# VectorE copies 24 columns of x per group instead of 12

## The chip, the core and the metric

The kernel runs on one core of a Trainium2 chip. The core has a matrix engine (TensorE, PE in the profile), a vector engine (VectorE, DVE), an activation engine (ScalarE, ACT), a general engine (GpSimd, POOL) and a queue engine (SyncE, SP). Each has its own instruction stream and they meet only at semaphores. The metric is device time in microseconds, from the first to the last instruction plus a little around them.

## What is computed

One graph layer with attention on edges, a batch norm and a layer norm. There are N = 12,500 nodes with 128 features and E = 212,500 edges, sorted by destination:

```python
Q, K, V = x @ WQ, x @ WK, x @ WV            # seen as 8 heads of 16
Eh = edge_attr @ WE
score = exp(clip(sum_over_head(K[src] * Q[dst] / 4 * Eh), -5, 5))
wV = segment_sum(V[src] * score, dst);  Z = segment_sum(score, dst)
h = x + wV / (Z + 1e-6)
y = batch_norm_over_nodes(h) * gamma + beta
out = layer_norm_over_features(x + y)
```

## The kernel before

The edges are cut into 1661 tiles of 128. Eight tiles make a group, and there are 208 groups. A window of 64 nodes holds the destinations of four tiles, so Q is not gathered: a 64-column piece of x is multiplied by WQ and spread to the edges with a one-hot matrix.

K and V of the sources do need a gather. At the start the kernel makes a table `kvd` of K and V for all nodes in DRAM (256 floats a row). For each tile, POOL issues one indirect DMA (L290, queue POOL) that brings 128 rows of it into the tile's part of a slot `slot` (9 slots of 8 tiles). Some groups have one tile, the eighth, that comes another way, and POOL then issues seven gathers for the group:

- 61 tiles by ACT: x lies transposed in SBUF as `hx`, one node a column. ACT copies 40 single columns a group (L393) into `xc`, PE multiplies 128 collected columns by `w_kv` (`cols_mm`, L430), ACT copies the product into the slot (`cols_out`, L435).
- 24 tiles by SP: 16 row DMAs a group (L411), copied into the slot by ACT (L421).
- 18 tiles by VectorE: 12 single columns a group (L366) into `xv`, and the same PE and ACT steps as for ACT's columns.

The column numbers are ids in SBUF (`v_ids`). One instruction of the sequencer (`load_v`, L357, TENSOR_LOAD in the profile) loads 12 of them into registers of VectorE; in front of every copy stands one register instruction (`ISA` in the program's order, FUSED_REGOPS in the profile) that turns a node number into an address. `v_plan` says at which groups a tile is collected and multiplied (`v_at`), and into which group's slot it goes (`v_tiles`).

The order of work is written out by hand: the program is one loop over groups g, and each engine runs its instructions in that order. On VectorE the order of a group is: four products K·Eh and ·Q (L800, two halves of four tiles each), the head sums (L807), the clip (L816), the one-hot of group g+2 (L748), three steps on group g-2 (L852, L855, L859), the one-hot of g+1 (L740, L741), and the message V·score (L822), which waits for ACT's exponential (L817), which waits for the clip. The 12 copies stand after L822. The id load stands between L807 and L816.

PE runs the edge products (L775), the spread of Q (L784), the sums over destinations (L843) and some small ones. POOL's gathers are issued in order; `pace` ties each to a step of the other engines, so that they are spread over a group. A gather into a slot can be issued once the message of the group that had the slot is done.

Of the kernel before, what the change touches and what calls it, by code (L numbers as in the profile page):

```python
# [15 lines left out]
ET = mybir.EngineType  # L16
# [22 lines left out]
FIRST_COL = 8  # L39
# [2 lines left out]
FIRST_ROW = 8  # L42
ROW_LAG = 2
NSEM = 6
V_COLS = 12


LAST = [3, 2]
# [51 lines left out]
def v_plan(sizes):  # L100
    full, used = sizes.count(U) // 2, set(col_plan(sizes) + row_plan(sizes))
    tiles, at, end = [], [], P
    while True:
        m = FIRST_COL + -(-end // V_COLS)
        while (m - FIRST_COL) * COLS % P < COLS:
# [17 lines left out]
def gnn_kernel(  # L123
# [19 lines left out]
    nc = tc.nc  # L143
    N, D = out.shape
# [131 lines left out]
    def slot(i):  # L276
        return rows.tile([P, 2 * G * P], F32, name=f"slot{i}")

    first = slot(NSLOT).rearrange("p (h c d) -> p h c d", h=2, d=2 * P)
# [21 lines left out]
    def issue(n=0):  # L301
        while len(queued) > n:
            f, *a = queued.pop(0)
            f(*a)
# [20 lines left out]
    tot_v = len(v_tiles) * P  # L325
    apart = set(col_tiles + row_tiles + v_tiles)
    v_ids = consts.tile([P, 2 * V_COLS], I32, name="v_ids")
    nc.vector.memset(v_ids, 0)
# [10 lines left out]
    def load_ids(to, n, first, total):  # L339
        m, rest = divmod(total, n)  # L340
        for p, k, w in ((0, m, n), (m, 1, rest)):
            if w and k:
                nc.sync.dma_start(to[p:p + k, :w], bass.AP(
                    tensor=rsrc.tensor, offset=rsrc.offset + first + n * p, ap=[[n, k], [1, w]]))

    def load_col_ids():
        load_ids(col_ids, 2 * COLS, 0, tot)
        load_ids(row_ids, 2 * SP_ROWS, tot, tot_rows)
        load_ids(v_ids, 2 * V_COLS, tot + tot_rows, tot_v)

    OFFV = {}

    def load_v(g):
        q = g - FIRST_COL
        if 0 <= q < -(-tot_v // V_COLS):
            at = q % 2 * V_COLS
            _, OFFV[g] = nc.values_load_multi_w_load_instructions(  # L357
                v_ids[q // 2:q // 2 + 1, at:at + V_COLS], engines=(ET.DVE,), min_val=0, max_val=N - 1,
                skip_runtime_bounds_check_because="node ids")

    def fetch_v(g):
        for r, off in zip(range((g - FIRST_COL) * V_COLS, tot_v), OFFV.get(g, ())):
            k = r // P
            if r % P == 0:
                XV[k] = wp.tile([P, P], F32, name="xv", bufs=2)
            nc.vector.tensor_copy(XV[k][:, r % P:r % P + 1], hx[:, ds(off, 1)])  # L366
# [8 lines left out]
    def load_cols(g):  # L375
        q = g - FIRST_COL
        if 0 <= q < -(-tot // COLS):
            at = q % 2 * COLS // 2
            _, words = nc.values_load_multi_w_load_instructions(
                col_pairs[q // 2:q // 2 + 1, at:at + COLS // 2], engines=(ET.Activation,), min_val=0,  # L380
                max_val=(N << 16) - 1, skip_runtime_bounds_check_because="node ids")
            OFFS[g] = [e for w in words for e in (w % (1 << 16), w >> 16)]
# [16 lines left out]
    def fetch_rows(g):  # L399
        q = g - FIRST_ROW  # L400
        if not 0 <= q < tot_rows // SP_ROWS:
            return
        c = q % 2 * SP_ROWS
        _, offs = nc.values_load_multi_w_load_instructions(
            row_ids[q // 2:q // 2 + 1, c:c + SP_ROWS], engines=(ET.SP,), min_val=0,
            max_val=(N - 1) * 8 * P, skip_runtime_bounds_check_because="node ids")
        for r, off in enumerate(offs, q * SP_ROWS):
            k = r // P
            if r % P == 0:
                BY_ROW[k] = late[0].tile([P, 2 * P], F32, name="byrow", bufs=2)  # L410
            d = nc.sync.dma_start(BY_ROW[k][r % P:r % P + 1, :].bitcast(U8), kvb[ds(off, 8 * P)].unsqueeze(0))  # L411
            d.then_inc(rows_in[k % NSEM], 16)
            tc.no_tile_sem_insts.add(d.ins.name)
            tc.add_to_no_dep_group(f"rows{k}", d.ins)
# [78 lines left out]
    def within(f, g):  # L493
        return f(g) if 0 <= g < NG else None
# [100 lines left out]
    def load_quad(q):  # L595
        t = late[0].tile([P, RQ, U * P], U8, name="rbq", bufs=2)
        for h in (0, 1):
            nc.sync.dma_start(t[h * WN:(h + 1) * WN].rearrange("p a b -> p (a b)"), places(h, RQ * q, RQ))
        for k in range(RQ):
            RB[RQ * q + k] = t[:, k, :]  # L600
# [93 lines left out]
    EA, OH, OT, XW, BASE, MSG, QE, OS, AT, AGG = ({} for _ in range(10))  # L694
# [4 lines left out]
    def halves(g):  # L699
        return [(0, usizes[2 * g]), (usizes[2 * g], nt(g))]  # L700

    def load(i):
        gs = range(2 * i, min(2 * i + 2, NG))
        if not gs:
            return
        t, n = wp.tile([P, 2, G, P], F32, name="ea", bufs=2), sum(nt(g) for g in gs)
        assert nt(2 * i) == G or len(gs) == 1
        for k, g in enumerate(gs):
            EA[g] = t[:, k]
        nc.sync.dma_start(t.rearrange("p c a b -> p (c a b)")[:, :n * P],  # L710
                          eaT[:, starts[2 * i] * P:(starts[2 * i] + n) * P])
# [83 lines left out]
    def products(g, hs=(0, 1)):  # L795
        for of in (EH, QE):
            for i in hs:
                a, b = halves(g)[i]
                kv = KV[g](a, b, 0)
                step = nc.vector.tensor_tensor(kv, kv, of[g][i][:, :b - a, :], op=OP.mult)  # L800
                PARTS.setdefault(g, []).append(step)

    def scores(g, h=None):
        if not h:
            SS[g] = wp.tile([P, G, H], F32, name="s", bufs=1)
        for a, b in ranges(g, h):
            step = nc.vector.tensor_reduce(SS[g][:, a:b, :], KV[g](a, b, 0).rearrange("p t (h d) -> p t h d", d=DH),  # L807
                                           axis=AX.X, op=OP.add)
        PARTS.setdefault(g, []).append(step)
# [128 lines left out]
    for q in range(NQ):  # L938
# [5 lines left out]
        for g, a in piece.get(q, []):  # L944
            if a == 0:
                i = free.pop(0)
# [62 lines left out]
    def share(g):  # L1009
        denom(g)  # L1010
        recip(g)
        attn(g)

    for g in range(NG - 2):
        within(load_rel, g + 3)
        if (g + 6) % RQ == 0 and (g + 6) // RQ in quads:
            load_quad((g + 6) // RQ)
        fetch_rows(g)
        if g % 2:
            load((g - 1) // 2 + 2)  # L1020
        within(products, g)
        within(scores, g)
        load_v(g)
        load_cols(g)
        fetch_cols(g, 0)
        within(clip_exp, g)
        within(turned_onehot, g + 2)
        if g >= 2:
            share(g - 2)
        late_x = g + 1 < nxg and g + 1 not in SLOT  # L1030
        if late_x:
            turn_x(g + 1, 0, True)
            turn_x(g + 1, 4, True)
            project_main(g + 1)
        within(eh_mm, g + 1)
        within(qe_mm, g + 1)
        cols_mm(g)
        paced = g >= LATE + 4
        if not paced:
            issue()  # L1040
        else:
            issue(G)
            for step in (SENT[g - 1], PARTS[g][1], BY["eh", g + 1], PARTS[g][3], PARTS[g][4], BY["qe", g + 1]):
                pace(step)
        within(onehot, g + 1)
        if paced:
            pace(BY["one", g + 1])
        within(message, g)
        fetch_cols(g, 1)
        within(q_window, g + 4)  # L1050
        cols_out(g)
        rows_out(g)
        fetch_v(g)
        within(add_x, g - 3)
        within(q_mm, g + 3)
        within(gather_sum, g - 1)
        if paced:
            pace(BY["sum", g - 1])
        within(x_out, g - 3)
        within(q_out, g + 3)  # L1060
        within(sums_out, g - 1)
        if g == 2:
            load_last()
            nc.vector.tensor_scalar(row_ids, row_ids, 8 * P, None, op0=OP.mult)
            pack_ids()
        if g % (RUN // 2) == 2 and g > 2 and (g // (RUN // 2) + 1) * SEC < T:
            load_section(g // (RUN // 2) + 1)
        for i, r in enumerate(runs):
            if i and g == placed[i]:
                place(r)  # L1070
        within_checks(g)
        while free and todo and todo[0] in done and not pending:
            load_x()
        bn_parts(2 * g - 7, 2 * g - 5)
        if g == NG - 4:
            assert done >= set(range(NPRE))
            norm_first()
        if g == LATE - 1:
            tps.close()
            late.append(tps.enter_context(tc.tile_pool(name="late", bufs=1)))  # L1080
        if g == LATE - 2:
            free.append(NSLOT)
            load_kv()
    last = NG - 1
    g = last - 1
# [336 lines left out]
```

## Time and profile before

| | us |
|---|---|
| median of 3 runs (lowest, highest) | 2026.02 (2023.14, 2029.82) |
| the profiled execution | 2024.75 |
| its span, first to last instruction | 2022.9 |
| busy: PE, PE's weight load, DVE, ACT, POOL | 1609.2, 1308.4, 1648.2, 1467.7, 1511.8 |
| mean granted clock of TensorE | 0.869 |

The profile gives, for each engine, the time in which it had an instruction in work. Register instructions, id loads and semaphore waits are not counted as busy, but a query of a line shows them (DVEq and ACTq are the sequencers of VectorE and ScalarE: the part that reads the instruction stream and hands instructions to the engine). In a timeline a row gives the start, the length and, in brackets, how long the engine had been idle and what ended that. A row of a line gives the count, the shortest, median and longest duration in ns, and the first and last start in us.

### The profile page before, as it was taken

The numbers are of one execution on the slowest core, as the hardware profiler recorded it, in microseconds if no ns is written. First come the engines' busy times: TensorE is split into PE (matmuls) and PEld (weight loads), VectorE is DVE, ScalarE is ACT, GpSimd is POOL, SyncE is SP. The second block draws the span as 40 slices with busy tenths as digits, with TensorE's granted clock in tenths as the row PEclk, the third lists the DMA queues.
The fourth block names the chain that finished last, engine by engine and source line by source line (L and its number), as shares of the span: only waits on it lengthen the run. The fifth ranks groups of instructions, "written<-read, shape, count | busy, mean of one in ns | idle before, by whom it ended". The sixth has DMA issues, their size and how long they took to land.

```text
span 2022.9 us, 65020 instructions
## 1 busy us (share of the span) xinstructions
PE 1609.2 (80%) x12891; PEld 1308.4 (65%) x12891; DVE 1648.2 (81%) x5264; ACT 1467.7 (73%) x9850; POOL 1511.8 (75%) x1594
## 2 busy tenths in 40 slices
PE   7888778887778887877888787778777777877787
PEld 7777666666666666665666666666566565665666
DVE  4468889889888988887888888788878788878887
ACT  2236878888788888777777777777777777777736
POOL 7677777777777777777777777777777777777765
PEclk9899888889888888888888888788888888888889
DMA  7855556556555656556656556556556556555664
GB/s 264 303 172 184 180 177 195 177 186 199 173 187 178 197 186 191 177 165 186 186 166 186 183 165 192 180 178 190 165 180 186 169 180 187 165 181 183 199 220 130
DMA packets 132237, 376.51 MB, mean 186 GB/s; under 512 B 37251, under 2 KB 50222, under 8 KB 117998
## 3 DMA queue, kind: packets, MB, share of 16 engines
q0 software_dynamic: 73760, 200.12, 33.8%
q1 hardware_dynamic: 54876, 171.03, 24.5%
q14 instruction: 312, 2.56, 0.4%
q8 instruction: 103, 1.69, 0.3%
q10 hardware_dynamic: 3186, 1.13, 0.2%
HBM read 346.69 MB, written 25.44 MB: 184 GB/s over the span
## 4 chain that ended last, share of the span: by engine, by line
issue 22%; DMA 19%; DVE 19%; PE 16%; ACT 15%; POOL 4%; ACTq 2%; DVEq 1%; SPq 1%; POOLq 0%
DMA slot<-kvd,srcs 17%; ACT xc L393 10%; DVE slot L800 7%; DVE s L807 5%; POOL slot L290 4%; PE ps_q L784 4%; PE ps_e L775 3%; PE ps_a L843 2%; DVE xv L366 2%; ACT ring L886 2%; DVE ot L748 1%; PE ps_e L487 1%; PE ps_q L910 1%; PE ps_e L910 1%; DVEq L366 1%
## 5 line engine op out<-in xcount | busy, mean ns | idle before, releaser
L290 POOL DMA_INDIRECT slot<-kvd,srcs x1494 | 1421.9, 952 | 459.9 <-issue 283.4
L393 ACT ACTIVATE xc<-hx 128x1 f32 x7808 | 1073.3, 201 | 248.2 <-issue 215.5
L775 PE MATMUL ps_e<-w_e,ea 128*128 128x128 f32 x3322 | 524.7, 313 | 269.7 <-DVE slot L800 209.1
L775 PEld LDWEIGHTS ps_e<-w_e,ea 128*128 128x128 f32 x3322 | 458.3, 216 | 335.3 <-DVE slot L800 243.5
L784 PE MATMUL ps_q<-qs,ot 64*128 64x128 f32 x3322 | 358.0, 340 | 84.6 <-DVE slot L800 74.2
L784 PEld LDWEIGHTS ps_q<-qs,ot 64*128 64x128 f32 x3322 | 294.6, 234 | 138.2 <-DVE slot L800 121.0
L800 DVE TENSOR_TENSOR slot<-slot,ps_e 128x512 f32<-128x512 f32 x410 | 268.1, 679 | 141.5 <-DMA slot<-kvd,srcs 125.0
L843 PE MATMUL ps_a<-msg,oh 128*64 128x136 f32 x3322 | 305.1, 307 | 1.7 <-DVE msg L822 1.7
L822 DVE TENSOR_TENSOR msg<-slot,ps_m 128x1024 f32<-128x1024 f32 (+2 forms) x209 | 248.7, 1191 | 34.9 <-ACT ps_m L817 32.6
L807 DVE TENSOR_REDUCE s<-slot 128x64 f32<-128x1024 f32 (+1 forms) x208 | 249.9, 1202 | 18.3 <-DVE slot L800 0.5
L800 DVE TENSOR_TENSOR slot<-slot,ps_q 128x512 f32<-128x512 f32 x410 | 261.6, 678 | 1.0 <-PE ps_q L784 0.7
L843 PEld LDWEIGHTS ps_a<-msg,oh 128*64 128x64 f32 x3322 | 194.5, 145 | 83.9 <-issue 61.6
L366 DVE COPY xv<-hx 128x1 f32 x2304 | 155.8, 143 | 0.0
L741 DVE TENSOR_TENSOR oh<-ps_i,rel 128x512 f32<-128x512 f32 x208 | 141.8, 682 | 0.0
L886 ACT ACTIVATE ring<-ps_a 128x64 f32 x408 | 90.5, 222 | 67.8 <-PE ps_a L843 46.4
L729 ACT ACTIVATE xw<-hx 128x64 f32 x416 | 83.6, 248 | 50.9 <-issue 36.3
L868 PE MATMUL ps_a<-ident,at 128*128 128x128 f32 x408 | 107.0, 350 | 1.2 <-ACT os L848 1.2
L817 ACT ACTIVATE ps_m<-s 128x64 f32<-128x64 f32 (+1 forms) x209 | 45.0, 215 | 76.6 <-DVE s L816 75.2
L868 PEld LDWEIGHTS ps_a<-ident,at 128*128 128x128 f32 x408 | 81.5, 227 | 28.3 <-issue 5.4
L748 DVE TENSOR_SCALAR ot<-rbq,wiota 128x512 f32<-128x512 uint8 x188 | 94.8, 504 | 0.0
L758 PE MATMUL ps_a<-w_q,xw 128*128 128x128 f32 x416 | 91.7, 307 | 0.4 <-ACT qs L762 0.4
L869 PE MATMUL ps_a<-xw,ident 128*128 128x128 f32 x408 | 90.8, 309 | 0.0
(188 smaller groups left out, 1492.2 us busy)
## 6 DMA issues: line engine op xcount, KB each, us to landing
ea<-eaT SPq DMA_DIRECT2D x103, 1024.0 KB
byrow<-kvd SPq DMA_DIRECT2D x3072, 1.0 KB
slot<-kvd,srcs POOLq DMA_INDIRECT x1494
rbq<-relT SPq DMA_DIRECT2D x94, 128.0 KB
kvd<-slot SPq DMA_DIRECT2D x12, 512.0 KB
kvd<-t SPq DMA_DIRECT2D x12, 512.0 KB
ring<-xT SPq DMA_DIRECT2D x24, 256.0 KB
hT<-ring SPq DMA_DIRECT2D x23, 256.0 KB
```

The costliest lines, as they stand in the source:

```text
L290: return nc.gpsimd.indirect_dma_start(out=out, out_offset=None, in_=table, in_offset=bass.IndirectOffsetOnAxis(ap=part(SRC, e, 1), axis=0))
L366: nc.vector.tensor_copy(XV[k][:, r % P:r % P + 1], hx[:, ds(off, 1)])
L393: nc.scalar.activation(XC[k][:, r % P:r % P + 1], column(at), AF.Copy)
L741: by(("one", g), nc.vector.tensor_tensor(one, iota_ps[:, None, :WN].to_broadcast([P, k, WN]), r[:, :, None].to_broadcast([P, k, WN]), op=O ...
L775: by(("eh", g), nc.tensor.matmul(t[:, j - a, :], EA[g][:, j, :], w_e, start=True, stop=True))
L784: by(("qe", g), nc.tensor.matmul(QE[g][h][:, j, :], OT[g][r, j * P:(j + 1) * P], QS[g][r], start=True, stop=True))
L800: step = nc.vector.tensor_tensor(kv, kv, of[g][i][:, :b - a, :], op=OP.mult)
L807: step = nc.vector.tensor_reduce(SS[g][:, a:b, :], KV[g](a, b, 0).rearrange("p t (h d) -> p t h d", d=DH), axis=AX.X, op=OP.add)
L822: step = nc.vector.tensor_tensor(MSG[g][:, a:b, :P].rearrange("p t (h d) -> p t h d", d=DH), KV[g](a, b, P).rearrange("p t (h d) -> p t h ...
L843: by(("sum", g), nc.tensor.matmul(AGG[g][h * WN:(h + 1) * WN], OH[g][h * n + j], MSG[g][:, h * n + j, :], start=(j == 0), stop=(j == k - 1)))
L868: nc.tensor.matmul(ps, AT[g], ident, start=True, stop=False)
L886: nc.scalar.activation(ring[:, ds(at, WN)], new, AF.Copy)
```

## The change

Three things are changed. `V_COLS` goes from 12 to 24, so that VectorE collects 24 columns in each of groups 8 to 199, and 36 tiles come in this way. The ids are loaded by two loads of 12 (`V_LOAD`); each stands right behind one of the two ·Q products, where before one stood behind the head sums. The copies stand in two batches of 12: one in the old place after the message, and a new one between the one-hot of g+2 and the steps on g-2.

```diff
-V_COLS = 12
+V_COLS = 24
+V_LOAD = 12
...
-    def load_v(g):
+    def load_v(g, half):
...
-            at = q % 2 * V_COLS
-            _, OFFV[g] = nc.values_load_multi_w_load_instructions(
-                v_ids[q // 2:q // 2 + 1, at:at + V_COLS], engines=(ET.DVE,), min_val=0, max_val=N - 1,
+            at = q % 2 * V_COLS + half * V_LOAD
+            _, OFFV[g, half] = nc.values_load_multi_w_load_instructions(
+                v_ids[q // 2:q // 2 + 1, at:at + V_LOAD], engines=(ET.DVE,), min_val=0, max_val=N - 1,
...
-    def fetch_v(g):
-        for r, off in zip(range((g - FIRST_COL) * V_COLS, tot_v), OFFV.get(g, ())):
+    def fetch_v(g, half):
+        first = (g - FIRST_COL) * V_COLS + half * V_LOAD
+        for r, off in zip(range(first, tot_v), OFFV.get((g, half), ())):
...
                 PARTS.setdefault(g, []).append(step)
+                if of is QE and len(hs) == 2:
+                    load_v(g, i)
...
         within(scores, g)
-        load_v(g)
         load_cols(g)
         fetch_cols(g, 0)
         within(clip_exp, g)
         within(turned_onehot, g + 2)
+        fetch_v(g, 0)
...
-        fetch_v(g)
+        fetch_v(g, 1)
```

The first place is on VectorE, in one group of the steady loop. Before, its order from the last products to the message is this (`ps_q` holds the spread Q, `s` the head sums, `ot`/`oh` one-hots):

```order
L800 TENSOR_TENSOR slot_22670<-slot_22670,ps_q 128x4x128 x2
L807 TENSOR_REDUCE s<-slot_22670 128x64
L357 TENSOR_LOAD v_ids
L816 TENSOR_SCALAR s<-s 128x64
L748 TENSOR_SCALAR ot<-rbq,wiota 128x512
L852 TENSOR_SCALAR rz<-os 128x8
L855 RECIPROCAL rz<-rz 128x8
L859 SCALAR_TENSOR_TENSOR at<-os,keep,rz 128x128
L740 TENSOR_TENSOR oh<-rel,lim 128x1
L741 TENSOR_TENSOR oh<-ps_i,rel 128x512
```

The same piece of a group after the change (line numbers are 2 to 4 higher; the pair of ISA and COPY, shown once, stands there 12 times):

```order
L802 TENSOR_TENSOR slot_25802<-slot_25802,ps_q 128x4x128
L358 TENSOR_LOAD v_ids
L802 TENSOR_TENSOR slot_25802<-slot_25802,ps_q 128x4x128
L358 TENSOR_LOAD v_ids
L811 TENSOR_REDUCE s<-slot_25802 128x64
L820 TENSOR_SCALAR s<-s 128x64
L750 TENSOR_SCALAR ot<-rbq,wiota 128x512
L368 ISA
L368 COPY xv<-hx 128x1
...
L856 TENSOR_SCALAR rz<-os 128x8
```

One load behind the head sums has become one behind each product, and 12 copies with 12 register instructions have come in ahead of the steps on g-2.

The second place is on POOL, at the gathers of groups 14 to 19, one row a group. Before:

```order
L290 DMA slot_1111<-kvd,srcs 128x256 x7
L290 DMA slot_1337<-kvd,srcs 128x256 x8
L290 DMA slot_1402<-kvd,srcs 128x256 x8
L290 DMA slot_1675<-kvd,srcs 128x256 x7
L290 DMA slot_1928<-kvd,srcs 128x256 x7
L290 DMA slot_2181<-kvd,srcs 128x256 x8
```

and after:

```order
L291 DMA slot_1111<-kvd,srcs 128x256 x7
L291 DMA slot_1337<-kvd,srcs 128x256 x8
L291 DMA slot_1402<-kvd,srcs 128x256 x7
L291 DMA slot_1712<-kvd,srcs 128x256 x7
L291 DMA slot_2001<-kvd,srcs 128x256 x7
L291 DMA slot_2291<-kvd,srcs 128x256 x8
```

The third row has gone from eight gathers to seven: group 16 is the first of the 18 that now get their eighth tile from VectorE's columns. Nothing else moves on POOL.

## The prediction

> **What bounds the kernel now.** I read the busy shares first, then the gathers of POOL over the whole span, then VectorE's waits by stretch, then one group of VectorE instruction by instruction. The page's shares do not name a bound:
>
> ```profile
> span 2022.9 us, 65020 instructions
> PE 1609.2 (80%) x12891; PEld 1308.4 (65%) x12891; DVE 1648.2 (81%) x5264; ACT 1467.7 (73%) x9850; POOL 1511.8 (75%) x1594
> ```
>
> POOL's 75% is misleading. Its gathers as a line (median ns, first and last start), and three of them in a timeline, with VectorE's 12 copies of that moment:
>
> ```profile
> L290 POOL DMA_INDIRECT slot<-kvd,srcs x1494: 940/946/1211, 90.0 to 1966.1; - x187
> ...
> 1013.23 0.94 POOL L290 DMA_INDIRECT slot<-kvd,srcs  x1 [0.30 <-issue]
> ...
> 1014.47 0.81 DVE L366 COPY xv<-hx 128x1 f32 x12
> 1014.47 0.94 POOL L290 DMA_INDIRECT slot<-kvd,srcs  x1 [0.30 <-issue]
> ...
> 1015.72 0.94 POOL L290 DMA_INDIRECT slot<-kvd,srcs  x1 [0.30 <-issue]
> ```
>
> A gather starts every 1.25 us. (1966.1 - 90.0) / 1493 = 1.257 us is the mean over the whole kernel, so POOL issues without a break from 90 us to 1966 us. That is the bound today. A group has 1494 / 207 = 7.22 gathers, 9.0 us. VectorE's side shows when this began to bite (70 messages from 300 to 900 us; then waits as total, times, longest, in 300 to 900 us; last row the same wait in 900 to 1900 us):
>
> ```profile
> L822 DVE TENSOR_TENSOR msg<-slot,ps_m x70: 1207/1220/1223, 302.8 to 899.7; 128x1024 f32<-128x1024 f32 x70
> DVE msg L822 <- ACT ps_m L817: 18.2, 32, 1.0
> DVE stats L889 <- ACT ring L886: 16.9, 8, 2.5
> DVE slot L800 <- DMA slot<-kvd,srcs: 6.3, 2, 4.1
> DVE relrow L583 <- PE ps_a L581: 4.6, 4, 2.0
> ...
> DVE slot L800 <- DMA slot<-kvd,srcs: 114.3, 62, 5.1
> ```
>
> Up to 900 us a group takes (899.7 - 302.8) / 69 = 8.65 us: the compute engines use up the lead of filled slots, and VectorE hardly waits for a gather. After that it waits 114.3 us for gathers. So POOL's lead over VectorE is small: 8.65 against 9.0. Without its four waits (46.0 us, 0.67 a group) VectorE needs **7.98 us a group** for its own chain. That is the number the change adds to.
>
> **The change part by part.**
>
> *Gathers.* 18 fewer at 1.25 us are 22.5 us off POOL; a group then has 1476 / 207 = 7.13, so 8.91 us. This is the whole possible gain, and it arrives only while VectorE's group stays under 8.91 us.
>
> *Where the new instructions fall.* One group of VectorE, and the records of its sequencer in the same group:
>
> ```profile
> 488.52 1.22 DVE L822 TENSOR_TENSOR msg<-slot,ps_m 128x1024 f32<-128x1024 f32 x1 [0.86 <-ACT ps_m L817]
> 489.66 0.81 DVE L366 COPY xv<-hx 128x1 f32 x12
> 490.38 1.27 DVE L800 TENSOR_TENSOR slot<-slot,ps_e 128x512 f32<-128x512 f32 x2
> 491.58 1.27 DVE L800 TENSOR_TENSOR slot<-slot,ps_q 128x512 f32<-128x512 f32 x2
> 492.95 1.22 DVE L807 TENSOR_REDUCE s<-slot 128x64 f32<-128x1024 f32 x1
> 494.21 0.19 DVE L816 TENSOR_SCALAR s<-s 128x64 f32<-128x64 f32 x1
> 494.32 0.48 DVE L748 TENSOR_SCALAR ot<-rbq,wiota 128x512 f32<-128x512 uint8 x1
> 494.71 0.37 DVE L852 TENSOR_SCALAR rz<-os 128x8 f32<-128x8 f32 x1
> ...
> 496.48 1.22 DVE L822 TENSOR_TENSOR msg<-slot,ps_m 128x1024 f32<-128x1024 f32 x1
> ```
>
> ```profile
> L366 DVEq FUSED_REGOPS  x12: 46/46/46, 488.5 to 489.8; - x12
> L366 DVE COPY xv<-hx x12: 143/144/146, 489.7 to 490.3; 128x1 f32 x12
> ...
> L800 DVEq EVENT_SEMAPHORE  x2: 21/21/21, 491.1 to 491.7; - x2
> L800 DVE TENSOR_TENSOR slot<-slot,ps_q x2: 677/678/679, 491.6 to 492.2; 128x512 f32<-128x512 f32 x2
> ...
> L357 DVEq TENSOR_LOAD <-v_ids x1: 870/870/870, 493.0 to 493.0; - x1
> ```
>
> Three things are to be seen. Copies run at a pitch of (490.3 - 489.7) / 11, about 0.06 us, but the sequencer prepares them at (489.8 - 488.5) / 11, about 0.115 us each. In the old place this is hidden: it prepares them from 488.5 on, while L822 runs for 1.22 us. And it starts on them only at 488.5, when L822 was released after 0.86 us of waiting for ACT: it does not run ahead past an instruction whose wait is open.
>
> *The old batch* stays as it is, under L822: no cost beyond what is in the 7.98.
>
> *The new batch* stands behind L816 and L748. L816 is released by L807's end, 494.21. The register work can begin about 0.1 us later, and its twelfth piece is done at 494.31 + 11 x 0.115 + 0.05 = 495.62, the copy starts at about 495.67. L852, which stood at 494.71, follows a copy's pitch later at 495.73: **+1.02 us**. The bounds: 12 x 0.06 = 0.73 if preparation were free; 12 x 0.115 = 1.38 if L816 and L748 hid nothing. I take 1.02, because both instructions (0.5 us up to L852) do hide the first four or five pieces. What may hide more is the wait for ACT's exponential, at L822 behind it (18.2 us in 70 groups, 0.26 a group): it goes, and is left out below.
>
> *The two loads.* Today's load takes 0.87 us wholly under L807 (1.22 us). What a load does to an engine's stream when nothing covers it is shown on ACT, whose load of 20 words stands behind short instructions:
>
> ```profile
> L379 ACTq TENSOR_LOAD <-col_pairs x1: 1298/1298/1298, 1017.9 to 1017.9; - x1
> ...
> 1018.08 0.29 ACT L848 ACTIVATE os<-ps_a 128x136 f32<-128x136 f32 x1
> 1019.38 0.77 ACT L393 ACTIVATE xc<-hx 128x1 f32 x5 [1.01 <-issue]
> ```
>
> What was handed over before (L848) still runs, the next waits until the load ends at 1019.2. On VectorE the first product's wait is passed at 491.1, its start is 491.58; the load lasts from about 491.19 to 492.06, the second product is due at 492.18 and is handed over in time: almost nothing lost. Its own load then runs from about 492.22 to 493.09, and the head sums start near 493.22 in place of 492.95: **+0.27 us**. Bounds: 0 if the sequencer ran ahead further, and 2 x (0.87 + 0.09) - 1.37 = 0.55 if each load began only with its product's start (0.09 is the step around a load, 1.37 the distance from 491.58 to 492.95). I take 0.27, since the wait at 491.1 is a row and not a guess. The removed load at L807 gives nothing back: L816 has to wait for L807 anyhow.
>
> *PE and ACT* get 18 more column products, in two parts of about 0.48 us each, and 18 copies of 0.384 us:
>
> ```profile
> L430 PE MATMUL ps_e<-w_kv,xv x36: 379/483/793, 260.1 to 1924.2; 128*128 128x256 f32 x36
> ...
> L435 ACT ACTIVATE slot<-ps_e x79: 384/384/386, 207.5 to 1950.3; 128x256 f32<-128x256 f32 x79
> ```
>
> That is 7 us of ACT and under 18 us of PE over 192 groups. I cost them at nothing: a longer VectorE group leaves both idle for 0.7 us or more a group. If that cover were gone they would cost 0.04 and 0.09 us a group.
>
> *Waits that stay.* Each of the 8 statistics steps waited 2.1 us for ACT's writes. Of that 1.02 goes to the new batch, and 0.3 because ACT, no longer late, starts at once: 0.8 x 8 / 69 = 0.09, with the 4.6 / 69 = 0.07 of L583 it is 0.16 us a group. The gather wait goes.
>
> **The sum.** A group of VectorE: 7.98 + 1.02 + 0.27 + 0.16 = 9.43 us, which is over POOL's 8.91. VectorE becomes the bound, and POOL, whose next gather needs a slot that VectorE has left, waits. Before, the groups that copy took (first and last copy of
>
> ```profile
> L366 DVE COPY xv<-hx x2304: 135/143/151, 172.3 to 1907.0; 128x1 f32 x192
> ```
>
> less 0.7 for the last batch itself) 1734.0 / 191 = 9.08 us. So 192 x (9.43 - 9.08) = +67 us. The last eight groups copy nothing and find their gathers done: they lose the late gather wait, 114.3 us over the 107 groups (1000 us / 9.36) of 900 to 1900 us, 1.07 each, -8.6 us. Net +58.6 us. The profiled execution took 2024.75 us, 1.85 more than its span and 1.3 under the median of the runs; put on the median, 2026.0 + 58.6 = **2085 us**.
>
> **The rivals.**
>
> *Faster: POOL stays the bound.* If VectorE's sequencer prepared copies and loaded ids past an open wait, the new batch would be ready when L807 ends and cost 0.73, the loads nothing. 7.98 + 0.73 + 0.16 = 8.87 us is under 8.91, and the gain of 22.5 us arrives: 2003 us. It decides at 8.91 - 8.14 = 0.77 us of new time a group. The rows at 488.5 speak against it: 0.86 us of open wait, and no preparation in it. [...]
>
> *Slower still: each load begins with its product.* 0.55 in place of 0.27 is 192 x 0.28 = +54 us, 2139 us. It holds if the wait of the first product is passed late, as where PE is behind; against it, the group above.
>
> [...] If copies held up POOL's gathers, each new batch would add up to 0.81 us to POOL's 8.91: 9.72 us, and POOL would be the bound again: 192 x (9.72 - 9.08) = +123, 2149 us. The gather at 1014.47 ran beside 12 copies and took 0.94 us, as its neighbours did. [...]
>
> *No change.* If the batch cost 0.9, the loads 0.1 and waits 0.1, the group takes 9.08, as before.
>
> **Chances.** My forecast, 2035 to 2115 us: 0.6. Loads in full and other waits, 2115 and above: 0.2, of it the port 0.03. POOL stays the bound: 0.1, since the row against it is plain, but stands in one wait on one instruction. Within 0.3% (about what a measurement of this kernel can tell from no change, 2020 to 2032 us): 0.07; between that and the forecast 0.03. Faster 0.1, same 0.07, slower 0.83. The range from 2024 to 2150 leaves out the faster case and some 0.08 at the top. The forecast's own range is from loads of 0.1 to 0.4 us.
>
> **What would show it.** After the change: gathers 1476, with pitches well over 1.25 us and waits on a slot; VectorE's wait for gathers near zero and its busy share up by some 156 us of copies (2304 at 67 ns) ahead of everything; from L820 to L856 1.5 us in place of 0.50; L811 0.27 us later after the products; ACT waiting for the clip before its exponential in most groups. I am wrong if L820 to L856 is near 1.2 us, if L822's old wait for ACT is still there, or if gathers still run at 1.25 us to the end.

## The result and the profile after

The changed kernel takes 2050.98 us (median of 4 runs, 2046.35 to 2053.71) against 2026.9 us: 1.0123 times the time before, 95% interval [1.0108, 1.0137], about 24 us slower. The prediction had the direction; its 2085 us is 34 us too long, a loss of 59 us where 24 came.

The page of the changed kernel, its profiled run, which took 2053.71 us; of the chain of work that ended last the shares by engine; and its groups of instructions (busy, mean ns of one, idle before):

```profile
span 2051.9 us, 69925 instructions
PE 1644.1 (80%) x12927; PEld 1334.3 (65%) x12927; DVE 1824.6 (89%) x7568; ACT 1482.1 (72%) x9868; POOL 1500.1 (73%) x1576
...
DVE 41%; issue 19%; DVEq 13%; PE 9%; DMA 5%; ACT 4%; POOL 1%; ACTq 1%; POOLq 0%
...
L368 DVE COPY xv<-hx 128x1 f32 x4608 | 359.5, 145 | 5.7 <-issue 5.3
L811 DVE TENSOR_REDUCE s<-slot 128x64 f32<-128x1024 f32 (+1 forms) x208 | 249.9, 1202 | 67.1 <-DVE slot L802 64.5
L826 DVE TENSOR_TENSOR msg<-slot,ps_m 128x1024 f32<-128x1024 f32 (+2 forms) x209 | 247.9, 1188 | 1.4 <-ACT ps_m L821 0.9
```

The same chain, the message and the head sums on the page of before:

```profile
issue 22%; DMA 19%; DVE 19%; PE 16%; ACT 15%; POOL 4%; ACTq 2%; DVEq 1%; SPq 1%; POOLq 0%
...
L822 DVE TENSOR_TENSOR msg<-slot,ps_m 128x1024 f32<-128x1024 f32 (+2 forms) x209 | 248.7, 1191 | 34.9 <-ACT ps_m L817 32.6
L807 DVE TENSOR_REDUCE s<-slot 128x64 f32<-128x1024 f32 (+1 forms) x208 | 249.9, 1202 | 18.3 <-DVE slot L800 0.5
```

VectorE is busy 89% of the span, and the chain that ended last is in the main VectorE and its sequencer (DVE and DVEq, 54% together, and 20% before). The idle time before the message, 34.9 us and nearly all for ACT before, is 1.4 us. Before the head sums 64.5 us of idle time now end with the product ahead of them, by the page (0.5 us before).

VectorE's waits from 300 to 1900 us after the change (total, times, longest):

```profile
DVE s L811 <- DVE slot L802: 58.0, 168, 0.7
DVE stats L893 <- ACT ring L890: 6.7, 7, 2.3
DVE relrow L585 <- PE ps_a L583: 5.3, 9, 0.6
DVE xv L368 <- issue: 5.1, 19, 0.3
```

There is no row for a gather any more (before: 6.3 and 114.3 us). The messages of that stretch, after:

```profile
L826 DVE TENSOR_TENSOR msg<-slot,ps_m x174: 1203/1210/1214, 302.2 to 1899.3; 128x1024 f32<-128x1024 f32 x174
```

and before:

```profile
L822 DVE TENSOR_TENSOR msg<-slot,ps_m x176: 1203/1210/1223, 302.8 to 1894.9; 128x1024 f32<-128x1024 f32 x176
```

A group takes (1899.3 - 302.2) / 173 = 9.23 us after and (1894.9 - 302.8) / 175 = 9.10 us before. One group of VectorE after the change:

```profile
488.64 1.33 DVE L802 TENSOR_TENSOR slot<-slot,ps_q 128x512 f32<-128x512 f32 x2
490.33 1.22 DVE L811 TENSOR_REDUCE s<-slot 128x64 f32<-128x1024 f32 x1 [0.36 <-DVE slot L802]
491.58 0.20 DVE L820 TENSOR_SCALAR s<-s 128x64 f32<-128x64 f32 x1
491.69 0.48 DVE L750 TENSOR_SCALAR ot<-rbq,wiota 128x512 f32<-128x512 uint8 x1
492.09 1.04 DVE L368 COPY xv<-hx 128x1 f32 x12
493.04 0.16 DVE L856 TENSOR_SCALAR rz<-os 128x8 f32<-128x8 f32 x1
...
494.48 1.21 DVE L826 TENSOR_TENSOR msg<-slot,ps_m 128x1024 f32<-128x1024 f32 x1
495.61 0.81 DVE L368 COPY xv<-hx 128x1 f32 x12
```

Twelve copies in the new place take 1.04 us, in the old place 0.81 us. From the clip (L820) to the first step on g-2 (L856) it is 1.46 us in place of 0.50. From the products' start to the head sums it is 1.69 us; before it was 1.37. The sequencer's records of the same group say why:

```profile
L358 DVEq TENSOR_LOAD <-v_ids x2: 866/868/870, 488.3 to 489.3; - x2
...
L802 DVEq EVENT_SEMAPHORE  x2: 21/21/21, 488.2 to 489.2; - x2
L802 DVE TENSOR_TENSOR slot<-slot,ps_q x2: 684/685/686, 488.6 to 489.3; 128x512 f32<-128x512 f32 x2
```

The first load runs from 488.3, ahead of its product's start, and ends at about 489.1, shortly before the second product is due. Only then does the sequencer come to the second product's semaphore (489.2), and behind that product to the second load, which runs from 489.3 to 490.17. The head sums, for which the engine is free at 490.0, start at 490.33.

### The profile page after: what moved, and what is told of

It reads as the page before. It is cut to its first block, busy times and chain, and to the rows that moved or that the text cites. A ratio compares the mean times of both kernels' runs of the same rounds, so it can differ in the third digit from the quotient of the medians.

```text
span 2051.9 us, 69925 instructions
## 1 busy us (share of the span) xinstructions
PE 1644.1 (80%) x12927; PEld 1334.3 (65%) x12927; DVE 1824.6 (89%) x7568; ACT 1482.1 (72%) x9868; POOL 1500.1 (73%) x1576
## 3 DMA queue, kind: packets, MB, share of 16 engines
q8 instruction: 103, 1.69, 0.3%
## 4 chain that ended last, share of the span: by engine, by line
DVE 41%; issue 19%; DVEq 13%; PE 9%; DMA 5%; ACT 4%; POOL 1%; ACTq 1%; POOLq 0%
DVE slot L802 12%; DVE xv L368 12%; DVE s L811 9%; DVEq L358 8%; DMA slot<-kvd,srcs 5%; DVEq L368 4%; PE ps_q L786 2%; PE ps_a L847 2%; ACT xc L395 2%; PE ps_e L777 1%; DVE rz L859 1%; DVE at L863 1%; DVE msg L826 1%; DVE oh L742 1%; POOL slot L291 1%
## 5 line engine op out<-in xcount | busy, mean ns | idle before, releaser
L777 PE MATMUL ps_e<-w_e,ea 128*128 128x128 f32 x3322 | 544.8, 320 | 318.3 <-DVE slot L802 180.4
L777 PEld LDWEIGHTS ps_e<-w_e,ea 128*128 128x128 f32 x3322 | 473.9, 222 | 386.9 <-DVE slot L802 206.8
L786 PE MATMUL ps_q<-qs,ot 64*128 64x128 f32 x3322 | 372.4, 346 | 19.8 <-DVE slot L802 11.7
L368 DVE COPY xv<-hx 128x1 f32 x4608 | 359.5, 145 | 5.7 <-issue 5.3
L786 PEld LDWEIGHTS ps_q<-qs,ot 64*128 64x128 f32 x3322 | 305.2, 240 | 80.1 <-DVE slot L802 67.2
L811 DVE TENSOR_REDUCE s<-slot 128x64 f32<-128x1024 f32 (+1 forms) x208 | 249.9, 1202 | 67.1 <-DVE slot L802 64.5
L802 DVE TENSOR_TENSOR slot<-slot,ps_q 128x512 f32<-128x512 f32 x410 | 270.6, 682 | 3.1 <-PE ps_e L777 1.1
L802 DVE TENSOR_TENSOR slot<-slot,ps_e 128x512 f32<-128x512 f32 x410 | 261.0, 677 | 6.1 <-ACT xw L731 5.6
L890 ACT ACTIVATE ring<-ps_a 128x64 f32 x408 | 90.5, 222 | 64.5 <-PE ps_a L847 46.0
L863 DVE SCALAR_TENSOR_TENSOR at<-os,keep,rz 128x128 f32<-128x128 f32 x208 | 73.0, 351 | 22.3 <-DVE rz L859 1.4
```

The lines of the kernel that those rows point to most:

```text
L777: by(("eh", g), nc.tensor.matmul(t[:, j - a, :], EA[g][:, j, :], w_e, start=True, stop=True))
L786: by(("qe", g), nc.tensor.matmul(QE[g][h][:, j, :], OT[g][r, j * P:(j + 1) * P], QS[g][r], start=True, stop=True))
```

## The experiments

The theory: VectorE has become the bound, its group has grown by about 1.0 us for the new batch, because the sequencer prepares a copy in about 0.115 us while the engine makes one in about 0.06, and by 0.3 us for the loads. The rivals: POOL still bounds, in stretches or because the copies hold up its gathers; PE and ACT with their 18 more products; ACT's late exponentials.

Three of the five sets of runs met chips on which the kernel before the change itself takes 2647 to 2678 us; in e5_loads_moved, one of them, 532 of ACT's 8723 register instructions take over 0.3 us (shown at the end). Those runs tell the parts of a VectorE group, and not what a change is worth in time.

### One part undone at a time

One load of 12 ids for both batches:

```diff
-                if of is QE and len(hs) == 2:
-                    load_v(g, i)
...
+        load_v(g, 0)
+        OFFV[g, 1] = OFFV.get((g, 0), ())
         load_cols(g)
```

> The changed kernel with one load of 12 ids, behind the head sums as before the change; both batches of copies use these 12 ids, so that the 18 added tiles hold columns of other nodes (that part of the result is left out). Theory (VectorE is the bound; the two loads stand in the open with 0.31 us a group: the head sums start 1.045 us after the last product in place of 0.78, the second product 0.04 us late): that step goes back to 0.78 us, VectorE's group goes from 9.24 to 8.93 us, which is POOL's 8.91, and the time from 2051 to 2005 to 2020 us. Rival 1 (the copies hold up POOL's gathers) and rival 2 (the 18 added products on PE and ACT): nothing that they rest on is changed, 2045 to 2055 us. Rival 3 (the new batch alone makes up the loss, loads are covered): 2045 to 2055 us.

Ratio to the kernel before 0.9974 [0.9961, 0.9986], on a chip with 2678 us before. In the timeline of VectorE the head sums are back at their old distance from the products, 1.39 us, and the new batch is as long as ever:

```profile
1004.82 1.28 DVE L802 TENSOR_TENSOR slot<-slot,ps_q 128x512 f32<-128x512 f32 x2
1006.21 1.22 DVE L809 TENSOR_REDUCE s<-slot 128x64 f32<-128x1024 f32 x1
...
1007.96 1.02 DVE L368 COPY xv<-hx 128x1 f32 x12
```

So the two loads are the 0.3 us before the head sums, and the page's releaser there ("DVE slot L802") is the place of the wait, not its cause.

Fixed columns in the new batch, so that no register instruction stands in front of a copy (the unused load of the first 12 ids goes with it):

```diff
-            nc.vector.tensor_copy(XV[k][:, r % P:r % P + 1], hx[:, ds(off, 1)])
+            at = hx[:, r:r + 1] if half == 0 else hx[:, ds(off, 1)]
+            nc.vector.tensor_copy(XV[k][:, r % P:r % P + 1], at)
```

> The changed kernel, but the 12 copies of the new batch take fixed columns, so that no register instruction stands in front of them (the 18 added tiles are not those of the reference). Theory (the batch costs 1.0 us a group because the sequencer prepares a copy in 0.115 us while the engine makes one in 0.06 us): the way from the clip to the first step on g-2 goes from 1.46 to about 1.22 us, VectorE's group to 9.0 us, the time to 2005 to 2020 us. [...]

Ratio 0.9921 [0.9903, 0.9938], same chip. VectorE's timeline:

```profile
1000.46 0.20 DVE L821 TENSOR_SCALAR s<-s 128x64 f32<-128x64 f32 x1
1000.57 0.65 DVE L751 TENSOR_SCALAR ot<-rbq,wiota 128x512 f32<-128x512 uint8 x1
1001.14 0.80 DVE L369 COPY xv<-hx 128x1 f32<-128x1 f32 x12
1001.86 0.35 DVE L857 TENSOR_SCALAR rz<-os 128x8 f32<-128x8 f32 x1
```

The same 12 copies now take 0.80 us, as under the message. The preparation is what makes them 1.04. From the clip to L857 it is 1.40 us in this group; L751 and L857 are longer here than in the group above. Over all groups the median is 1.235 us against 1.458, 0.22 us less where some 0.24 were expected; had the copies themselves taken the 1.0 us, it would have stayed at 1.46.

18 tiles gathered by POOL again, the columns' products put aside:

```diff
-    apart = set(col_tiles + row_tiles + v_tiles)
+    apart = set(col_tiles + row_tiles + v_tiles[::2])
+    unused = set(v_tiles[1::2])
...
+            if k in unused:
+                nc.scalar.activation(spare_out, PAIRS[g], AF.Copy)
+                return
```

> The changed kernel with 18 of its 36 tiles gathered by POOL again; VectorE still collects all columns, PE multiplies them, and ACT puts 18 of the products where nobody reads them. POOL has its 1494 gathers back, 9.0 us a group. Theory (VectorE bounds with 9.24 us a group): no change, 2045 to 2057 us, and POOL's idle time shrinks by about 22 us. Rival (POOL is still the bound in stretches): up to 18 x 1.25 = 22.5 us more, 2065 to 2074 us.

Ratio 1.007 [1.0051, 1.0088]; what the changed kernel takes on that chip was not run, so nothing follows.

The loads moved, everything computed:

```diff
-                if of is QE and len(hs) == 2:
-                    load_v(g, i)
+                if of is EH and len(hs) == 2 and i:
+                    load_v(g, 0)
...
         within(scores, g)
+        load_v(g, 1)
         load_cols(g)
```

> The changed kernel with only the id loads moved: the first behind the second edge product, where two products of 0.6 us each are still ahead of it in the queue, the second behind the head sums, as before the change. Everything is computed. Theory: both loads are covered, VectorE's group loses the 0.31 us (9.24 to 8.93 us) and POOL, at 8.91 us, is as much the bound: 2005 to 2020 us, faster than before the change by up to 1%. Rival (a load costs its time on VectorE wherever it stands): 2045 to 2055 us.

Ratio 0.9989 [0.9978, 1.0001]; nothing told of the time. The steps from product to product and to the head sums have medians of 0.604 and 0.783 us, as before the change (0.598 and 0.782): both loads are covered.

The loads moved as above and, besides, the new batch:

```diff
         within(products, g)
+        fetch_v(g, 0)
         within(scores, g)
...
         within(turned_onehot, g + 2)
-        fetch_v(g, 0)
```

> Everything is computed. The id loads moved as in the run before (the first behind the second edge product, the second behind the head sums) and the new batch of copies moved from behind the clip to behind the last product, ahead of the head sums, where 1.2 us of products are still in the queue while the sequencer prepares it. Theory, on a chip where POOL's pitch and VectorE are the two bounds (as in the traces of before and after): the loads cost nothing, the batch only its copies at 0.06 us, 0.75 us in place of 1.0, so VectorE's group is 9.24 - 0.31 - 0.25 = 8.7 us, under POOL's 8.91; POOL is the bound and its 18 gathers less count: 2003 to 2010 us against 2027 before the change, ratio 0.989 to 0.992. Rival (the copies cost their preparation wherever they stand): 2030 us or more. On a chip where register instructions of ACT take 0.7 us now and then, as in the runs before, ACT bounds and both theories expect a ratio of 0.99 to 1.0 with nothing told; there only the way from the last product to the head sums speaks: 0.78 + 0.75 us by the theory, 0.78 + 1.0 or more by the rival.

Ratio 0.9967 [0.9955, 0.9979], on a chip with 2647 us before. From the last product to the head sums, with the batch now between them, the median is 1.33 us, 0.55 more than the 0.78 without it; the expectation had 0.75 more, its rival 1.0.

### ACT and SP taken out of the question

To be free of those chips, and to test the rival of ACT's late exponentials, ACT's columns and SP's rows were fixed in four kernels (their tiles then hold rows of other nodes):

```diff
-            nc.scalar.activation(XC[k][:, r % P:r % P + 1], column(at), AF.Copy)
+            nc.scalar.activation(XC[k][:, r % P:r % P + 1], hx[:, r:r + 1], AF.Copy)
...
-            d = nc.sync.dma_start(BY_ROW[k][r % P:r % P + 1, :].bitcast(U8), kvb[ds(off, 8 * P)].unsqueeze(0))
+            d = nc.sync.dma_start(BY_ROW[k][r % P:r % P + 1, :].bitcast(U8), kvb[r * 8 * P:(r + 1) * 8 * P].unsqueeze(0))
```

> The kernel before, but ACT's 61 tiles take fixed columns and SP's 24 tiles fixed rows, so that neither has an id to load or an address to prepare (those 85 tiles are not those of the reference; transfers, copies and their sizes are the same). It is the base for the next three, which have the same edit. All theories: POOL issues its 1494 gathers without a break, 1.25 us apart, and the time is 2010 to 2050 us also on a chip where register instructions of ACT and SP stall; if it is over 2200 us, something else of that chip bounds, and the four runs tell only their parts of a group.

> The changed kernel with fixed columns on ACT and fixed rows on SP. Theory (VectorE becomes the bound, with 1.0 us a group for the new batch and 0.31 us for the loads): 20 to 35 us over the base f0_before, VectorE's group 9.1 to 9.3 us with hardly a wait for gathers or for ACT. Rival (ACT, with its 18 more copies and late exponentials, is what makes the changed kernel slower): ACT now has half its work, so the gain of 18 gathers arrives, 15 to 22 us under f0_before.

> f1_after with the id loads and the new batch moved, as in the run with both moves. Theory: VectorE's group is 8.5 to 8.7 us, POOL bounds with 18 gathers less: 15 to 23 us under f0_before. Rival (24 copies are too much for VectorE wherever they stand): as f1_after.

> f1_after with the id loads alone moved. Theory: VectorE's group loses 0.31 us, 8.9 to 9.0 us, as long as POOL's 8.91: 5 to 20 us under f0_before, 30 to 50 under f1_after. Rival (the loads cost nothing in the changed kernel): as f1_after.

They ran on a chip like the first, all against a kernel before of 2022.66 us:

| run | us | ratio to the kernel before |
|---|---|---|
| f0_before | 2024.3 | 1.0003 [0.9992, 1.0014] |
| f1_after | 2039.76 | 1.0079 [1.0056, 1.0102] |
| f2_both | 2000.25 | 0.9883 [0.9862, 0.9904] |
| f3_loads | 1996.82 | 0.9867 [0.985, 0.9884] |

f0_before, in which ACT is busy 1122.2 us in place of 1467.7, takes what the kernel before takes: ACT is no bound there. f1_after is 15.5 us slower than its base, less than the 20 that was expected, and far from the rival's gain: most of the loss does not come by ACT. Not all of it is accounted for. The real change has a ratio of 1.0123 [1.0108, 1.0137], f1_after 1.0079 [1.0056, 1.0102], and the two intervals do not meet; some 9 us of the 24 may come by the ids on ACT and SP, or by the other chip, and no run separates these. (From the message of group 8 to that of group 200 it is 24.5 us longer, 1767.9 against 1743.4; the end is 12 us shorter, with the gathers long done.) Moving the loads alone (f3_loads) takes off 43 us, which is 0.22 us in each of 192 groups, and the gain of the 18 gathers appears: 27.5 us under f0_before. That is more than the 5 to 20 that were expected, and more than 18 gathers are worth (22.5); in the two profiles the gathers also start 1.9 us earlier and follow each other 2 ns sooner, 3 us over all of them; why is open. f2_both, with the batch moved too, is 24 us under f0_before, no better than f3_loads.

### POOL, VectorE's own chain, and the real kernels again

The first repetition of three kernels met a chip with 2649.64 us before:

> The changed kernel with only the id loads moved, everything computed, the same kernel as e5_loads_moved, taken again because that run met a chip on which ACT's register instructions bound every kernel. On a chip as in the first traces, theory: VectorE's group 8.95 to 9.0 us, 1995 to 2008 us, ratio to the kernel before 0.983 to 0.992. Rival (ACT's real ids and late exponentials cost what fixed columns hid): as the changed kernel, ratio 1.005 to 1.013.

> Loads and new batch moved, everything computed, the same kernel as e6_both. On a chip as in the first traces, theory: POOL bounds with 18 gathers less, 1998 to 2008 us, ratio 0.985 to 0.992. Rival: the new batch ahead of the head sums delays the exponential so far that VectorE waits for ACT again, ratio over 0.995.

> The changed kernel with 18 of its 36 tiles gathered by POOL again and the products of their columns put where nobody reads them, the same kernel as e3_gathers_back. On a chip as in the first traces, theory (VectorE bounds with 9.24 us a group, POOL with 9.0 us has room): as the changed kernel within 6 us, ratio to the kernel before 1.009 to 1.016. Rival (POOL is still the bound in stretches): up to 22.5 us more than the changed kernel, ratio 1.018 to 1.024.

0.9985 [0.9972, 0.9999], 0.9982 [0.9967, 0.9997] and 1.0079 [1.0055, 1.0103]: inconclusive for the question. The next four were on a chip like the first, with 2021.83 us before. h0_own_chain is f0_before with, in each group from 18 on, one gather issued as a plain transfer by SP:

```diff
+            plain = g >= 2 * NSLOT and sizes[g] == G
+            if plain:
+                nc.sync.dma_start(KV[g](0, 1, 0, 2 * P)[:, 0, :], kvd[:P, :])
-            for j in range(sizes[g] - (g in apart)):
+            for j in range(plain, sizes[g] - (g in apart)):
```

> The base f0_before (fixed columns on ACT, fixed rows on SP), and in each group from 18 on one of POOL's gathers is a plain transfer of the same size issued by SP (those tiles hold other rows). POOL needs some 7.8 us a group, so that VectorE with its 12 copies is the bound. Theory (the chain was over-estimated: 7.64 us of core steps and 0.2 us of others, 7.86): the group takes 7.8 to 7.95 us, the time falls to 1800 to 1840 us. Rival (the chain is 7.98 us and more, as predicted, and the change's parts cost less than they seem): 8.0 to 8.3 us, 1840 to 1890 us.

> f1_after with 18 of the 36 tiles gathered by POOL again, and the products of their columns put where nobody reads them. Theory (VectorE bounds with 9.2 us a group, POOL with 9.0 has room): within 6 us of f1_after, ratio to the kernel before 1.005 to 1.011. Rival (POOL is still the bound in stretches): up to 22.5 us more, ratio 1.014 to 1.019.

> The changed kernel with the id loads moved, everything computed. On a chip as in the first traces: ratio 0.983 to 0.992 by the theory, 1.005 to 1.013 by the rival that ACT's real ids take the gain. On a chip where ACT's register instructions bound: 0.996 to 1.0, which tells nothing.

> Loads and new batch moved, everything computed. On a chip as in the first traces: ratio 0.985 to 0.992 by the theory; over 0.995 if the later exponential makes VectorE wait for ACT. On a chip where ACT's register instructions bound: 0.996 to 1.0, which tells nothing.

| run | us | ratio to the kernel before |
|---|---|---|
| h0_own_chain | 1792.39 | 0.8866 [0.8848, 0.8883] |
| h1_gathers_back | 2040.15 | 1.0097 [1.0076, 1.0117] |
| h2_loads_moved | 2003.66 | 0.9913 [0.9893, 0.9933] |
| h3_both | 2002.93 | 0.9905 [0.9885, 0.9925] |

The messages of h0_own_chain from 300 to 1500 us:

```profile
L825 DVE TENSOR_TENSOR msg<-slot,ps_m x153: 1209/1210/1215, 300.4 to 1495.4; 128x1024 f32<-128x1024 f32 x153
```

and what VectorE waits for in it from 300 to 1700 us:

```profile
DVE relrow L586 <- PE ps_a L584: 5.9, 11, 0.7
DVE slot L803 <- DMA slot<-kvd,srcs: 3.7, 3, 2.1
DVE stats L892 <- ACT ring L889: 1.8, 3, 1.1
```

With POOL relieved a group of VectorE takes (1495.4 - 300.4) / 152 = 7.86 us, small waits included, and not 7.98. POOL still issues its 1303 gathers 1.26 us apart, but VectorE waits 3.7 us for them in all of this stretch. The time fell 8 us further than was expected. It also says how firmly POOL held the kernel before: one gather less a group is worth 11%.

h1_gathers_back gives POOL its 18 gathers back and takes what f1_after takes (1.0097 and 1.0079, intervals overlapping, where the rival asked for 1.014 or more): with 24 copies POOL no longer bounds. Its gathers and those of f1_after:

```profile
L291 POOL DMA_INDIRECT slot<-kvd,srcs x1494: 942/946/1206, 90.4 to 1968.6; - x187
```

```profile
L291 POOL DMA_INDIRECT slot<-kvd,srcs x1476: 942/946/1212, 88.3 to 1943.6; - x185
```

POOL ends 25 us later, and the kernel with it gains or loses nothing.

h2_loads_moved and h3_both compute everything and are faster than both kernels, by 0.9% against before; against the changed kernel that is some 2% (0.9913 / 1.0123, worked out over two sets of runs). The timeline of VectorE in h2, then in h3:

```profile
486.92 1.28 DVE L802 TENSOR_TENSOR slot<-slot,ps_q 128x512 f32<-128x512 f32 x2
488.30 1.22 DVE L811 TENSOR_REDUCE s<-slot 128x64 f32<-128x1024 f32 x1
489.56 0.20 DVE L820 TENSOR_SCALAR s<-s 128x64 f32<-128x64 f32 x1
...
491.01 0.33 DVE L856 TENSOR_SCALAR rz<-os 128x8 f32<-128x8 f32 x1
```

```profile
488.55 1.28 DVE L802 TENSOR_TENSOR slot<-slot,ps_q 128x512 f32<-128x512 f32 x2
489.75 0.81 DVE L368 COPY xv<-hx 128x1 f32 x12
490.48 1.21 DVE L811 TENSOR_REDUCE s<-slot 128x64 f32<-128x1024 f32 x1
```

and VectorE's waits in h3 from 900 to 1900 us:

```profile
DVE slot L802 <- DMA slot<-kvd,srcs: 26.2, 21, 3.2
DVE stats L893 <- ACT ring L890: 21.4, 13, 3.1
```

In h2 the head sums are 1.38 us behind the products' start again. In h3 the batch takes 0.81 us, and the head sums start 1.93 us after the products' start, 0.55 more than in h2: the copies push them back by 0.73 us (490.48 - 489.75), of which 0.18 were lost between product and sums anyhow. The way from the clip to L856 is back at 0.5 us in h3, so VectorE saves 0.4 us a group against h2. In time it brings nothing that can be measured: the last rows show VectorE waiting for gathers again, and longer for the statistics. The 18 gathers less are all there is to gain, 22.5 us; 18 to 19 have come.

## Why the prediction was right in direction and wrong in size

*What bounds the kernel now* was right: POOL before; h0_own_chain shows it. But the share of a group was taken wrongly. The 1494 gathers were divided by 207 groups, while the first eight groups have gathers of their own, in a row that the prediction does not show:

```profile
L290 POOL DMA_INDIRECT slot<-x,srcs x64: 940/944/1292, 3.1 to 84.3; - x64
```

So the 1494 serve 200 groups. That is 7.47 a group and 7.47 x 1.257 = 9.39 us, and VectorE's group from 900 to 1900 us, 9.38 us, fits it. With 1476 it is 7.38 and 9.28 us, not 8.91. The mean of 9.08 is shorter because VectorE first used up filled slots: from the start of a group's last gather to the group's message it is, by the trace, 72 us at group 8 and 11 at group 80. What VectorE's group has to stay under for the whole gain is this mean less the 18 gathers, (1741.9 - 22.5) / 192 = 8.96 us; that it is close to 8.91 is luck.

*The new batch*, +1.02 us: right. From the clip to the steps on g-2 the mean over all groups is 1.55 us after and 0.53 before, +1.01. The reason given for it, preparation at 0.115 us a copy, is shown by the fixed columns of e2_fixed (0.22 us less).

*The two loads*, +0.27 us: right. The second product comes 0.05 us late, the head sums 0.26 us, together 0.31; e1_one_load and e5_loads_moved take it away.

*PE and ACT at nothing*: not contradicted. h2_loads_moved has all 18 products and their copies and still gains 18 of the 22.5 us; what of the 9 us above goes by ACT in the changed kernel is open.

*VectorE's own chain of 7.98 us*, with the 0.16 us of *waits that stay* added to it, is the step that failed: 8.14 us. h0_own_chain measures 7.86 us with its small waits included, and the changed kernel itself, less the two new parts, leaves 9.23 - 1.01 - 0.31 = 7.91. The 7.98 was made by taking four rows of waits from 8.65 us, in a stretch in which VectorE and ACT kept each other waiting. The smaller rows of waits of that stretch stayed in it, 3.2 us or 0.05 a group, and so did longer steps: the one-hot ahead of the message, the first step on g-2 and the 12 copies together take some 0.1 us a group more there than in h0_own_chain. 7.86 + 1.01 + 0.31 = 9.18, and the group took 9.23 us, so that hardly 0.05 was left for waits. The prediction had 9.43. 0.2 us of 9.4 is 2%, but the loss is the difference to the 9.08 before, and 192 x 0.2 = 38 us of the forecast's 67 was this error. Both ends of the range were bounded by the new parts alone; the base had no bounds. That the 2050.98 us lie inside the range of 2035 to 2115 is luck: its low end stood for cheaper loads, and the loads cost what was forecast.

*The last groups*, -8.6 us: from the message of group 200 to the end it is 109.8 us before and 106.3 after, -3.5 us. The sum with the measured terms: from the message of group 8 to that of group 200 1772.9 against 1741.9 us, +31.0; the tail -3.5; the start +1.5; together the 29.0 us between the two spans.

The rival *POOL stays the bound* fell as it was argued. In the profile after, a load starts before its product (488.3 and 488.64), so there the sequencer ran ahead of an instruction that waited for the engine. It did not run ahead of one whose semaphore was open: the clip waits for the head sums until 491.58, and the first register instruction of the new batch starts at 491.6, though the head sums had been handed over at 490.3.

The rival that copies hold up POOL's gathers, *the port* of the chances: no run shows such a port. The median gather is 949 ns after and 946 before, 3 ns of 1.25 us, and 946 in f1_after with the same 24 copies.

Of the signs that were named, VectorE's wait for gathers went, and so did the message's wait for ACT. ACT waited for the clip in 82 of the 174 groups from 300 to 1900 us, about half and not most. And one sign of being wrong came: the gathers still run at one pitch to the end, from 90.7 to 1950.0 us, (1950.0 - 90.7) / 1475 = 1.26 us, although POOL had stopped bounding. The corrected share explains it. POOL's own group of 7.38 x 1.26 = 9.30 us is no shorter than VectorE's 9.23, so VectorE does not fall behind POOL; the lead of filled slots, which before was used up, stays (73 us at group 8, 63 at group 80, 57 at group 200). So POOL's pitch did not tell that it had stopped bounding; the distance from its last gather to the end did (57 us before, 102 after).

## What to carry to other kernels

When work is moved from one engine that bounds to another that is nearly as long, the result is the difference of two group times; measure the second engine's own group with the first relieved before pricing anything, since 2% of it can be half of the answer. And count over the groups that really have the work: 1494 gathers over 207 groups or over 200 is 9.0 or 9.4 us.

In this kernel a copy with register work in front of it cost the engine's 0.06 us where a long instruction covered the preparation (12 took 0.81 us under the message of 1.21), and up to the sequencer's 0.115 us in the open (12 took 1.04 us). An id load of 0.87 us cost nothing that shows where work handed over before outlasted it, two products of 0.6 us or the head sums of 1.22; two loads, one behind each ·Q product, cost 0.31 us a group. Moving the two loads alone turned a loss of 1.2% into a gain of 0.9%, with all 24 copies in place; moving the batch as well brought nothing more that could be measured, and moving the batch alone was not run.

## What the runs showed of the hardware that was not expected

The chips of these runs differ. The register instructions of ACT in front of its column copies, with the time for which ACT's copies waited for nothing the profile shows, in e5_loads_moved (a chip on which the kernel before takes 2678 us) and then in h2_loads_moved, the same program (2022 us):

```profile
L395 ACTq FUSED_REGOPS  x7808: 3/76/1437, 251.2 to 2595.3; - x196
L395 ACT ACTIVATE xc<-hx x7808: 185/203/206, 251.4 to 2595.4; 128x1 f32 x196
...
  issue: 670.2, 1025
```

```profile
L395 ACTq FUSED_REGOPS  x7808: 73/77/95, 166.6 to 1920.8; - x196
L395 ACT ACTIVATE xc<-hx x7808: 185/203/206, 166.7 to 1920.9; 128x1 f32 x196
...
  issue: 215.6, 297
```

The median is the same, but on the first chip 532 of ACT's 8723 register instructions take over 0.3 us, most of them 0.7 us, 362 us in all; on SP it is 562 of 3074, on VectorE 24 of 4608, and none on ACT, SP or VectorE in h2_loads_moved. ACT's copies themselves take a median of 203 ns in both. The stalls of ACT add some 320 us (362 less 532 at 0.077), and the kernel takes 671 us longer, so they are not the whole of it. PE too waits there for nothing that the profile shows, first e5_loads_moved and then h2_loads_moved:

```profile
L847 PE MATMUL ps_a<-msg,oh 128*64 128x136 f32 x3322 | 349.0, 306 | 203.6 <-issue 201.0
```

```profile
L847 PE MATMUL ps_a<-msg,oh 128*64 128x136 f32 x3322 | 297.2, 301 | 1.7 <-DVE msg L826 1.7
```

and its granted clock is 0.79 in place of 0.88. That ACT is what bounds every kernel there, as the expectations of some later runs have it, is therefore not shown, and the cause stays open. On such a chip the two kernels that gain 0.9% elsewhere gain 0.1 to 0.3%.
